# Expert layers: choosing beside weighing and collecting, norms turned over 128 columns with a power on GpSimd, weights in four tiles

## Chip, cores and metric

The kernel runs on one core of a Trainium2 chip. The time is device microseconds of one execution of the whole program; lower is better. A core has TensorE (PE; its weight loads are listed as PEld), VectorE (DVE), ScalarE (ACT), GpSimd (POOL) and SyncE (SP), whose queue issues the DMAs of this kernel.

## The reference, cut to what matters

Four layers work on x of shape (4, 128, 64, 64), that is 4 images of 128 channels and 4096 tokens. Layers 2 and 3 end in a layer of experts each. Only these two are touched by the change. Here `t` is x as tokens (4, 4096, 128):

```
t = t + attention(_ln_t(t));  t = t + _ffn_ref(_ln_t(t))        # layers 2 and 3

def _ln_t(v, eps=1e-5): return (v - mean(v)) / sqrt(var(v) + eps)   # over 128 channels

def _ffn_ref(x, gate_w, gate_b, weight1, weight2):              # E=64 experts, H=512, K=8
    probs = softmax(x @ gate_w.T + gate_b, axis=1)              # over the 4096 tokens
    vals, idx = top_k(probs, 8)                                 # per image and expert
    pooled = sum_k x[idx_k] * vals_k
    h = gelu([pooled, 1] @ weight1[e]);  out = [h, 1] @ weight2[e]
    outputs[idx_k] += out * vals_k
```

Each expert picks its eight likeliest tokens of an image, sums them with their probabilities, runs a small network on the sum and adds the answer back to those tokens. The weights of a layer are 64 x (128 x 512 + 512 x 128) floats, 33.6 MB, each used once.

## The kernel before, in words

`expert_ffn` (L1703) is called twice, from the top function (L2057), once after layer 2's attention and once after layer 3's. The images stand in SBUF as four tiles of 128 channels by 4096 tokens. Two images make a pair `pr`; the 64 experts of one image and the 64 of the other fill the 128 partitions.

`weigh(pr)` (L1762) takes the tokens in 8 chunks of 512 columns, the two images of a pair in turn, so 16 steps `n`. `centred` multiplies by a centring matrix and squares on ScalarE. `deviation` multiplies the squares by a matrix of 1/128 (L91 is the line of every such matmul), so that every partition holds the variance; VectorE turns 64 partitions of 512 columns in blocks of 32 (L1782), ScalarE takes the square root of one column of each block (L1784), VectorE inverts (L1785) and turns a broadcast back (L1786) into `rs`, the inverse deviation of each token. `gates` multiplies the two images by the gates' weights and VectorE scales by `rs` (L1796) into `pick`.

`choose(pr)` (L1800) works on all 4096 columns of `pick` at once: add the bias (L1803), the eight largest (L1805), exponential with its sum on ScalarE (L1809), share of the sum (L1812), the eight largest again (L1814), replace these by zero in a copy (L1816), subtract, so that only the eight remain (L1817), and multiply them by `rs` into `pick_rs` (L1818).

`collect(pr)` (L1820) turns, chunk by chunk, `pick_rs` and both images so that tokens are on partitions (12 transposes, three copies to SBUF), and sums picked tokens by matmuls into `pool`; its tail puts the sums into `pooled`.

The calls are weigh(0); choose(0); weigh(1) interleaved with collect(0); choose(1); collect(1). `run` steps generators in turn and `in_turn` shifts the stages of a loop against each other by one step. That sets the order in which instructions are given; within `expert_ffn` a scheduler then sorts them on each engine by its own costs (only the attention of layer 2 has an order written out by hand).

Then come 16 groups of four experts: `hidden` (matmuls with `w1`, gelu), `turn_hidden`, `answer` (matmuls with `w2`), `place` (into `out_ps`). `expert_weights(g)` issues one DMA of 1 MB for `w1` and four of 256 KB for `w2`; each of the two has two buffers, groups 0 and 1 are loaded at the start and group g+2 once group g no longer needs its buffers. All DMAs stand in SP's queue in order, and an issue also waits for the DMA eight before it. At the end `out_s` is multiplied back onto the picked tokens and added to x (L1925).

`Common.layernorm_steps` (L99), used by the attention layers, has a turning over 128 columns already (L113 to L121): four variance matmuls of 32 rows, one turning of 128 columns, and four transposes on TensorE; its records serve as rows for such operations. GpSimd rows come from other layers too (L915, L1271, L1611).

Of the kernel before, what the change touches and what calls it, by code (L numbers as in the profile page):

```python
# [17 lines left out]
P = 128  # L18
# [3 lines left out]
CH = 512  # L22
# [8 lines left out]
class Common:  # L31
# [3 lines left out]
    def __init__(self, tc, pool):  # L35
# [6 lines left out]
        def const(name, shape, value):  # L42
            t = pool.tile(shape, F32, name=name)
            nc.vector.memset(t, value)
            return t
# [7 lines left out]
        nc.vector.tensor_tensor(self.center, self.ident, self.mean, ALU.subtract)  # L53
        self.eps5 = const("eps5", [P, 1], 1e-5)
        self.half_pi = const("half_pi", [P, 1], math.pi / 2)

# [33 lines left out]
    def mm(self, out, lhsT, rhs, start=True, stop=True):  # L90
        self.nc.tensor.matmul(out, lhsT, rhs, start=start, stop=stop)  # L91
# [7 lines left out]
    def layernorm_steps(self, out, terms, work, psum, affine=None, bufs=2):  # L99
# [22 lines left out]
        if affine is None:  # L122
            nc.vector.tensor_tensor(out, kept, vp, ALU.mult)
        else:
            nc.vector.scalar_tensor_tensor(kept, kept, g, vp, ALU.mult, ALU.mult)
            nc.gpsimd.tensor_scalar(out, kept, b, None, ALU.add)

    def later(self, f, *args, **kw):
# [971 lines left out]
def run(*parts):  # L1100
    for _ in in_turns(*parts):
        pass
# [600 lines left out]
def expert_ffn(K, xs, w, tag):  # L1703
# [10 lines left out]
    with ExitStack() as ctx:  # L1714
        pool = lambda name, bufs, **kw: ctx.enter_context(tc.tile_pool(reuse_waits="tile", name=f"{tag}_{name}", bufs=bufs, **kw))
        cst = pool("const", 1)
        wts = pool("wts", 2)
        tok = pool("tok", 1)
        work = pool("work", 2)
# [3 lines left out]
        def expert_weights(g):  # L1723
            es = slice(g * GE, (g + 1) * GE)
            w1 = wts.tile([P, GE, HID], F32, name="w1")
            nc.sync.dma_start(out=w1, in_=w["weight1"][es, 0:P, :].rearrange("e d h -> d e h"))
            w2 = wts.tile([P, GE, NHC, P], F32, name="w2")
            for e in range(GE):
                nc.sync.dma_start(
                    out=w2[:, e], in_=w["weight2"][g * GE + e, 0:HID, :].rearrange("(k p) o -> p k o", p=P)  # L1730
                )
            return w1, w2
# [8 lines left out]
        nc.sync.dma_start(out=b2, in_=w["weight2"][:, HID, :])  # L1741
        ahead = [expert_weights(g) for g in range(2)]
        gp = psum.tile([P, NE], F32, name="gate_ps", tag="mm")
# [15 lines left out]
        picks = [cst.tile([P, L], F32, name=f"pick{pr}") for pr in range(2)]  # L1759
        parts = {}  # L1760

        def weigh(pr):  # L1762

            pb = picks[pr]
            rs = parts[pr] = tok.tile([P, L], F32, name="rs")
            sqs = {}

            def src(n):
                return xs[2 * pr + n % 2][:, n // 2 * CH : n // 2 * CH + CH]

            def centred(n):
                xc = psum.tile([P, CH], F32, name="ln_xc", tag="mm")
                mm(xc, K.center, src(n))
                sqs[n] = work.tile([P, CH], F32, name="ln_sq")
                nc.scalar.activation(sqs[n], xc, AF.Square)

            def deviation(n):
                half, cols = slice(64 * (n % 2), 64 * (n % 2) + 64), slice(n // 2 * CH, n // 2 * CH + CH)
                vp = psum.tile([P, CH], F32, name="ln_var", tag="mm")
                mm(vp, K.mean, sqs[n])  # L1780
                vt = work.tile([P, CH // 32, 32], F32, name="ln_vt")
                nc.vector.transpose(vt[half].rearrange("p a b -> p (a b)"), vp[half])  # L1782
                sd = work.tile([P, CH // 32, 1], F32, name="ln_sd")
                nc.scalar.activation(sd[half], vt[half, :, 0:1], AF.Sqrt, bias=K.eps5[half])  # L1784
                nc.vector.reciprocal(sd[half], sd[half])  # L1785
                nc.vector.transpose(  # L1786
                    rs[half, cols].rearrange("p (a b) -> p a b", b=32), sd[half].to_broadcast([64, CH // 32, 32])
                )

            def gates(n):  # L1790
                if n % 2:
                    lp = psum.tile([P, CH], F32, name="logits", tag="mm")
                    for h in range(2):
                        mm(lp[64 * h : 64 * h + 64, :], gate, src(n - 1 + h))
                    cols = slice(n // 2 * CH, n // 2 * CH + CH)
                    nc.vector.tensor_tensor(pb[:, cols], lp, rs[:, cols], ALU.mult)  # L1796

            return in_turn(2 * NCH, centred, deviation, gates)

        def choose(pr):  # L1800

            pb, rs = picks[pr], parts[pr]
            nc.vector.tensor_scalar(pb, pb, gate_b, None, ALU.add)  # L1803
            top = work.tile([P, 8], F32, name="top")
            nc.vector.max(top, pb)  # L1805
            nmx = work.tile([P, 1], F32, name="nmx")
            nc.vector.tensor_scalar(nmx, top[:, 0:1], -1.0, None, ALU.mult)
            tot = work.tile([P, 1], F32, name="tot")
            nc.scalar.activation(pb, pb, AF.Exp, bias=nmx, accum_out=tot)  # L1809
            rt = work.tile([P, 1], F32, name="rt")  # L1810
            nc.vector.reciprocal(rt, tot)
            nc.vector.tensor_scalar(pb, pb, rt, None, ALU.mult)  # L1812
            top = work.tile([P, 8], F32, name="top")
            nc.vector.max(top, pb)  # L1814
            ws = parts[pr] = tok.tile([P, L], F32, name="pick_rs")
            nc.vector.match_replace(ws, top, pb, 0.0)  # L1816
            nc.vector.tensor_tensor(pb, pb, ws, ALU.subtract)  # L1817
            nc.vector.tensor_tensor(ws, pb, rs, ALU.mult)  # L1818

        def collect(pr):  # L1820
# [27 lines left out]
            ps = work.tile([P, P], F32, name="pool_s")  # L1848
            nc.vector.tensor_copy(ps, pl)
            tp = psum.tile([P, P], F32, name="pool_t", tag="mm")  # L1850
# [10 lines left out]
        run(weigh(0))  # L1861
        choose(0)
        run(weigh(1), collect(0))
        choose(1)
        run(collect(1))


# [5 lines left out]
        def hidden(g):  # L1873
            w1, _ = ahead[g]
            hp = psum.tile([P, HID], F32, name="hid_ps", tag="mm")
            for j in range(GE):
                mm(hp[group(j), :], pooled[:, NB * (g * GE + j) : NB * (g * GE + j) + 32], w1[:, j, :], start=True, stop=False)
            for j in range(GE):
                mm(hp[group(j), :], one(g * GE + j), b1, start=False, stop=True)
            hid = hids[g] = work.tile([P, HID], F32, name="hid", tag="tok0")  # L1880
            nc.scalar.activation(hid, hp, AF.Gelu)
# [8 lines left out]
        def answer(g):  # L1890
# [8 lines left out]
            nc.vector.tensor_copy(a, ap)  # L1899
            if g + 2 < NG:  # L1900
                ahead.append(expert_weights(g + 2))

# [12 lines left out]
        for pr in range(2):  # L1915
            os_ = work.tile([P, P], F32, name="out_s")
            nc.vector.tensor_copy(os_, ops[pr])
            for c in range(NCH):
# [215 lines left out]
```

## Time and profile before

| what | value |
|---|---|
| median of 3 runs | 9885.43 us (9885.13 to 9886.97) |
| profiled execution, its time | 9881.09 us |
| its span | 9879.3 us |
| mean granted clock of TensorE | 0.920 |
| busy share PE / DVE / ACT / POOL | 88% / 73% / 75% / 49% |
| first expert layer, from the gates' weights to the last x | 8786 to 9132 us |
| attention of layer 3 | 9132 to 9517 us |
| second expert layer | 9517 to 9868 us |

The profile is one execution. Its rows give, for a group of instructions, the line, the engine, the operation with output and inputs, the count, busy time and the mean of one, and then the idle time just before them and what ended it. The timeline gives start, duration and idle time of single instructions, the stretches give busy time of each engine between two moments, the granted clock of TensorE (1 is full) and what the DMA engines moved. The second expert layer, in the stretch view (us, PE, PEld, DVE, ACT and POOL busy, clock, DMA share, GB/s), by the same stages as those that the prediction shows of the first:

```profile
9517.30:9568.00 50.70, 42.98 (x99) 13.28 (x99) 32.54 (x59) 15.70 (x34) 0.25 (x2) 0.94 0.22 66
9568.00:9600.70 32.70, 0.00 (x0) 0.00 (x0) 27.19 (x10) 5.08 (x3) 0.00 (x0) 0.54 0.00 0
9600.70:9667.00 66.30, 59.59 (x321) 30.52 (x321) 38.08 (x67) 24.97 (x50) 0.00 (x0) 0.97 0.00 1
9667.00:9698.30 31.30, 0.00 (x0) 0.00 (x0) 27.17 (x10) 3.80 (x2) 0.00 (x0) 0.54 0.00 0
9698.30:9728.00 29.70, 27.79 (x231) 21.04 (x233) 6.12 (x10) 9.90 (x18) 0.00 (x0) 0.91 0.01 1
9728.00:9847.00 119.00, 96.61 (x1088) 42.05 (x1088) 16.01 (x34) 9.89 (x17) 0.00 (x0) 0.76 0.83 248
```

### The profile page before, as it was taken

To read this page: it belongs to the slowest core of one execution; us is meant where nothing else is said; L and a number is where in the kernel's file an instruction comes from. 1 tells how busy PE (TensorE), PEld (TensorE's weight loads), DVE (VectorE), ACT (ScalarE), POOL (GpSimd) and SP (SyncE) were. 2 spreads that over 40 slices of the span, in tenths; PEclk is the share of its full clock that TensorE was granted. 3 is DMA by queue.
4 is the path that set the end of the run, shared out by engine and by line. 5 is a ranking of instruction groups with operands and counts; after the bars stand their busy time and mean duration, and the time that the engine had idled before them with its cause. 6 is when DMAs were issued, how large, how long until landed. Compare 5 with 4: busy or idle time off the path is not lost.

```text
span 9879.3 us, 187787 instructions
## 1 busy us (share of the span) xinstructions
PE 8736.1 (88%) x74074; PEld 3348.6 (34%) x74074; DVE 7220.5 (73%) x7877; ACT 7410.6 (75%) x10669; POOL 4802.8 (49%) x3175
## 2 busy tenths in 40 slices
PE   5888888888869999989999989999989999967776
PEld 2222222244523333333333333333333333333433
DVE  2889897988658888758888758888758888743463
ACT  3766767654359999879999879999879999841531
POOL 1677676765435555455555455555455555420000
PEclk8887878889979999989999989999989999988997
DMA  4524435223121221231111131211131211124004
GB/s 116 124 69 118 97 83 125 67 76 88 46 70 40 40 40 41 48 94 39 40 39 41 46 97 39 40 40 39 44 101 39 39 40 39 40 93 121 1 18 154
DMA packets 575731, 635.31 MB, mean 64 GB/s; under 512 B 113080, under 2 KB 369152, under 8 KB 573824
## 3 DMA queue, kind: packets, MB, share of 16 engines
q1 hardware_dynamic: 574848, 623.30, 25.6%
q8 instruction: 584, 9.57, 0.4%
q14 instruction: 299, 2.45, 0.1%
HBM read 446.84 MB, written 109.07 MB: 56 GB/s over the span
## 4 chain that ended last, share of the span: by engine, by line
PE 69%; DVE 10%; POOL 6%; ACT 5%; DMA 4%; issue 3%; SPq 2%; DVEq 0%; POOLq 0%; ACTq 0%
PE ctx_ps L91 27%; PE acc_ps L91 13%; PE score L91 11%; PE conv L91 4%; DVE hs L912 3%; POOL hs L916 3%; PE ln_xc L91 2%; PE y_ps L91 2%; DVE hs L901 2%; PE xc_ps L91 1%; DMA w<-in_L_ffn_weight 1%; PE ln_var L91 1%; PE b_ps L91 1%; PE hid_ps L91 1%; PE kv L91 1%
## 5 line engine op out<-in xcount | busy, mean ns | idle before, releaser
L1535 ACT ACTIVATE ex<-score 128x1024 f32<-128x1024 f32 x5120 | 4925.4, 1036 | 218.5 <-PE score L91 125.7
L91 PE MATMUL ctx_ps<-ex,qt 128*32 128x512 f32 x20480 | 2733.9, 606 | 19.9 <-DVE ctx L1469 19.9
L1484 POOL TENSOR_TENSOR folded<-ex 128x1024 f32<-128x1024 f32 x512 | 1224.2, 2391 | 2101.5 <-ACT ex L1535 1836.6
L1541 DVE STREAM_TRANSPOSE turned<-ex 128x1024 f32<-128x1024 f32 x1536 | 1885.8, 1228 | 329.1 <-ACT ex L1535 328.7
L1517 DVE STREAM_TRANSPOSE turned<-ex 128x1024 f32<-128x1024 f32 x1532 | 1842.4, 1203 | 0.0
L91 PE MATMUL acc_ps<-turned,turned_v 128*32 128x256 f32 x24576 | 1769.5, 379 | 3.1 <-POOL qt L1229 2.3
L912 DVE TENSOR_TENSOR_SCAN hs<-decay,carry,hs 128x512 f32<-128x512 f32 x1024 | 1245.7, 1266 | 193.6 <-ACT decay L908 180.1
L91 PE MATMUL score<-queries,keys 32*128 32x512 f32 x10240 | 1335.3, 497 | 44.0 <-POOL queries L1219 37.9
L91 PEld LDWEIGHTS acc_ps<-turned,turned_v 128*32 128x32 f32 x24576 | 800.9, 110 | 1476.5 <-issue 1323.8
L916 POOL TENSOR_TENSOR hs<-hs,c_sb 128x1024 f32<-128x1024 f32 x512 | 1207.3, 2358 | 81.4 <-DMA c_sb<-c_d 40.3
L908 ACT ACTIVATE decay<-dt,a_neg 128x512 f32<-128x512 f32 x1024 | 693.0, 689 | 662.5 <-DVE hs L912 653.3
L91 PEld LDWEIGHTS score<-queries,keys 32*128 32x128 f32 x10240 | 512.6, 182 | 1139.2 <-ACT ex L1535 780.9
L1347 POOL TENSOR_TENSOR turned_v<-v,quarter 128x1024 f32<-128x1024 f32 x256 | 612.4, 2393 | 265.7 <-PE acc_ps L91 225.0
L91 PE MATMUL y_ps<-hs,pair 128*64 128x512 f32 x2048 | 661.5, 773 | 33.6 <-POOL hs L916 33.6
L1485 POOL TENSOR_TENSOR quarters<-folded 128x512 f32<-128x512 f32 x512 | 657.7, 1285 | 40.2
L91 PEld LDWEIGHTS ctx_ps<-ex,qt 128*32 128x32 f32 x20480 | 406.4, 108 | 654.7 <-issue 598.7
L901 DVE TENSOR_TENSOR hs<-dtx,b_ps 128x2048 f32<-128x2048 f32 x256 | 580.1, 2266 | 55.9 <-PE b_ps L91 31.6
L91 PE MATMUL b_ps<-dbc,state 32*64 32x512 f32 x1024 | 343.2, 752 | 233.4 <-DVE hs L901 233.2
L1535 ACT ACTIVATION_READ_ACCUMULATOR ex<-score 128x1 f32 x2048 | 435.9, 213 | 0.0
L915 POOL COPY carry<-hs 128x2 f32<-128x2 f32 x512 | 98.1, 192 | 673.4 <-DVE hs L912 652.0
L1469 DVE COPY ctx<-ctx_ps 128x512 f32<-128x512 f32 x256 | 176.9, 691 | 329.3 <-PE ctx_ps L91 327.0
L1526 DVE TENSOR_REDUCE dacc<-quarters 128x2 f32<-128x512 f32 x508 | 327.1, 644 | 0.0
(371 smaller groups left out, 9016.1 us busy)
## 6 DMA issues: line engine op xcount, KB each, us to landing
c_sb<-c_d SPq DMA_DIRECT2D x512, 128.0 KB
queries<-head_d SPq DMA_DIRECT2D x1024, 64.0 KB
keys<-head_d SPq DMA_DIRECT2D x1024, 64.0 KB
under<-image_d SPq DMA_DIRECT2D x192, 264.0 KB
dt<-dt SPq DMA_DIRECT2D x128, 256.0 KB
dtx<-dtx SPq DMA_DIRECT2D x128, 256.0 KB
v<-value_d SPq DMA_DIRECT2D x1024, 32.0 KB
w<-in_L_ffn_weight SPq DMA_DIRECT2D x32, 1024.0 KB
```

The costliest lines, as they stand in the source:

```text
L91: self.nc.tensor.matmul(out, lhsT, rhs, start=start, stop=stop)
L901: nc.vector.tensor_tensor(hs, dtx2, bb.unsqueeze(1).to_broadcast([P, NQ, CH]), ALU.mult)
L908: nc.scalar.activation(ex, dt2[:, q, :], AF.Exp, scale=a_neg[:, q, g : g + 1])
L912: nc.vector.tensor_tensor_scan(hs[:, q, :], decays[q - 2 * i], hs[:, q, :], carry[:, g, q : q + 1], ALU.mult, ALU.add)
L916: nc.gpsimd.tensor_tensor(hs[:, two, :], hs[:, two, :], cs.unsqueeze(1).to_broadcast([P, 2, CH]), ALU.mult)
L1347: nc.gpsimd.tensor_tensor(t, v.unsqueeze(2).to_broadcast([P, 4 * BT, 4, HD]), quarter.unsqueeze(1).to_broadcast([P, 4 * BT, 4, HD]), ALU.mult,
L1484: nc.gpsimd.tensor_tensor(hs, exs[:, :, 0], exs[:, :, 1], ALU.add)
L1485: nc.gpsimd.tensor_tensor(qs, hs[:, :, 0 : CH // 2], hs[:, :, CH // 2 :], ALU.add)
L1517: nc.vector.transpose(*upright)
L1526: nc.vector.tensor_reduce(at, qs, AX.X, ALU.add)
L1535: nc.scalar.activation(ex, sps[p], AF.Exp, scale=scale, accum_out=sums[:, t : t + 1] if summed else None)
L1541: nc.vector.transpose(*upright)
```

## The change

Four things change, all in `expert_ffn`. Norms: `deviation` works on a chunk of both images; eight variance matmuls of 32 rows put the variances of 2 x 512 tokens on 128 partitions by 256 columns, one turning on VectorE, an add of the epsilon, a power of -1/2 on GpSimd and a broadcast copy there; a new stage `spreaded` transposes on TensorE and copies to `rs` on ScalarE. Choices: the bias goes into the exponential, the share into the copies `pool_s` and `out_s`, the second maximum is an exponential of the first; subtraction and product go chunk by chunk, the last two chunks on GpSimd; the function yields between its steps and runs beside weigh(1) and collect(0). Weights: one tile for both weights of a group, four such tiles, which also serve `rs` and `ws`; groups 1, 2 and 3 are loaded around collect(1), then g+4 after group g. A constant `minus_half` is added, and a helper `inverse_root`, which nothing calls.

```diff
         def weigh(pr):
-            rs = parts[pr] = tok.tile([P, L], F32, name="rs")
+            rs = parts[pr] = store.tile([P, L], F32, name="rs", tag="rs", bufs=2)
...
+            def deviation(c):
+                vp = psum.tile([P, 2, P], F32, name="ln_var", tag="mm")
+                for h, sq in enumerate(sqs.pop(c)):
+                    for k in range(4):
+                        mm(vp[32 * k : 32 * k + 32, h, :], K.mean[:, 0:32], sq[:, P * k : P * k + P])
+                vt = work.tile([P, 8, 32], F32, name="ln_vt")
+                nc.vector.transpose(vt.rearrange("p a b -> p (a b)"), vp.rearrange("p h s -> p (h s)"))
+                sd = work.tile([P, 4, 2], F32, name="ln_sd")
+                nc.vector.tensor_scalar(
+                    sd.rearrange("p k h -> p h k"), vt.rearrange("p (h k) i -> p h k i", h=2)[:, :, :, 0], 1e-5, None, ALU.add
                 )
+                flat = sd.rearrange("p k h -> p (k h)")
+                nc.gpsimd.tensor_tensor(flat, flat, K.minus_half[:, 0:8], ALU.pow)
+                wide = sds[c] = work.tile([P, 4, 2, 64], F32, name="ln_wide")
+                nc.gpsimd.tensor_copy(wide, sd.unsqueeze(3).to_broadcast([P, 4, 2, 64]))
+
+            def spreaded(c):
+                wide = sds.pop(c)
+                rp = psum.tile([P, CH], F32, name="ln_rs", tag="mm")
+                by_block = rp.rearrange("p (g b i) -> p b g i", b=4, i=32)
+                for k in range(4):
+                    nc.tensor.transpose(by_block[:, k], wide[:, k].rearrange("p h e -> p (h e)"), K.ident)
+                nc.scalar.copy(rs[:, c * CH : (c + 1) * CH], rp)
...
+            return in_turn(NCH, centred, deviation, spreaded, gates)
         def choose(pr):
             pb, rs = picks[pr], parts[pr]
-            nc.vector.tensor_scalar(pb, pb, gate_b, None, ALU.add)
             top = work.tile([P, 8], F32, name="top")
             nc.vector.max(top, pb)
...
+            yield
+            peak = work.tile([P, 1], F32, name="peak")
+            nc.vector.tensor_scalar(peak, top[:, 0:1], gate_b, None, ALU.add)
+            nc.vector.tensor_tensor(peak, gate_b, peak, ALU.subtract)
             tot = work.tile([P, 1], F32, name="tot")
...
+            nc.scalar.activation(top, top, AF.Exp, bias=peak)
+            nc.scalar.activation(pb, pb, AF.Exp, bias=peak, accum_out=tot)
+            nc.vector.reciprocal(shares[pr], tot)
+            yield
+            ws = store.tile([P, L], F32, name="ws", tag="b")
             nc.vector.match_replace(ws, top, pb, 0.0)
...
+            yield
+            for c in range(NCH):
+                cols = slice(c * CH, c * CH + CH)
+                engine = nc.vector if c < 6 else nc.gpsimd
+                engine.tensor_tensor(pb[:, cols], pb[:, cols], ws[:, cols], ALU.subtract)
+                engine.tensor_tensor(rs[:, cols], pb[:, cols], rs[:, cols], ALU.mult)
+                if c % 2:
+                    yield
...
         run(weigh(0))
-        choose(0)
-        run(weigh(1), collect(0))
-        choose(1)
+        run(weigh(1), choose(0))
+        run(choose(1), collect(0))
+        ahead[1] = expert_weights(1)
+        ahead[2] = expert_weights(2)
         run(collect(1))
+        ahead[3] = expert_weights(3)
...
         def expert_weights(g):
             es = slice(g * GE, (g + 1) * GE)
-            w1 = wts.tile([P, GE, HID], F32, name="w1")
+            t = store.tile([P, L], F32, name="w", tag=("a", "b", "rs", "rs")[g % 4], bufs=1 + g % 4 // 2)
+            w1 = t[:, 0 : GE * HID].rearrange("p (e h) -> p e h", e=GE)
...
-            if g + 2 < NG:
-                ahead.append(expert_weights(g + 2))
+            if g + 4 < NG:
+                ahead[g + 4] = expert_weights(g + 4)
```

## The prediction

> **What bounds the kernel now.** I read the page first: the span is 9879.3 us in a profiled execution of 9881.09 us (1.8 us lie around the span), and the shown runs have a median of 9885.43 us, 4.3 us above it. The program's instruction order on every engine is the same in both kernels up to the first expert layer, and again in the attention between the two expert layers, except for one small constant. So only two stretches count: 8762 to 9132 us and 9517 to 9868 us. I cut the first with the busy-time-by-stretch view (us, then PE, PEld, DVE, ACT, POOL busy, clock, DMA share, GB/s):
>
> ```profile
> 8786.50:8837.40 50.90, 43.19 (x100) 13.35 (x99) 32.44 (x58) 14.42 (x33) 0.00 (x0) 0.94 0.27 78
> 8837.40:8869.90 32.50, 0.00 (x0) 0.00 (x0) 27.05 (x10) 5.08 (x3) 0.00 (x0) 0.54 0.00 0
> 8869.90:8936.70 66.80, 59.66 (x321) 30.53 (x321) 38.14 (x68) 23.69 (x49) 0.00 (x0) 0.97 0.00 1
> 8936.70:8969.30 32.60, 0.00 (x0) 0.00 (x0) 27.16 (x10) 5.08 (x3) 0.00 (x0) 0.54 0.00 0
> 8969.30:8998.30 29.00, 27.06 (x227) 20.37 (x227) 6.14 (x11) 9.84 (x18) 0.00 (x0) 0.93 0.00 1
> 8998.30:9113.50 115.20, 95.23 (x1088) 41.94 (x1088) 15.74 (x33) 9.95 (x17) 0.00 (x0) 0.76 0.86 259
> ```
>
> The rows are weigh(0), choose(0), weigh(1) with collect(0), choose(1), collect(1), and the 16 groups of experts. In both choices TensorE does nothing for 32.5 us: VectorE alone carries the stage. Where weighing runs, TensorE is the limit (43 of 51, 60 of 67 us). The second expert layer repeats it: 50.7, 32.7, 66.3, 31.3, 29.7 and 119.0 us. The waits of these stretches, then four-microsecond stretches and the timeline inside the groups:
>
> ```profile
> PE tok_t L1830 <- DVE pick_rs L1818: 68.4, 2, 34.7
> ```
> ```profile
> PE hid_ps L91 <- DMA w<-in_L_ffn_weight: 18.6, 6, 4.1
> ```
> ```profile
> 9016.00:9020.00 4.00, 0.58 (x4) 0.23 (x8) 0.00 (x0) 0.00 (x0) 0.00 (x0) 0.72 1.14 334
> ...
> 9024.00:9028.00 4.00, 4.00 (x47) 2.43 (x40) 0.98 (x2) 0.00 (x0) 0.00 (x0) 0.50 0.43 129
> ```
> ```profile
> 9048.57 0.66 PE L91 MATMUL out_ps<-ans,spread 128*64 128x128 f32 x8
> ...
> 9051.26 1.35 PE L91 MATMUL hid_ps<-w,pooled 128*32 128x512 f32 x8 [2.03 <-DMA w<-in_L_ffn_weight]
> ...
> 9052.55 1.93 PE L91 MATMUL hid_ps<-b,ident 64*32 64x512 f32 x8
> ...
> 9057.90 1.04 PE L91 MATMUL out_ps<-ans,spread 128*64 128x128 f32 x8
> ...
> 9058.87 1.06 PE L91 MATMUL hid_ps<-w,pooled 128*32 128x512 f32 x8
> ```
>
> TensorE waits for weights every second group, and then works at half clock (1.93 us for what takes 1.06): the waits show 18.6 us, the half clock costs more. While TensorE works at half clock the loads stop (129 GB/s), since only two groups have a place. With loads queued they run at 330 GB/s (334, 326, 334, 336 in such stretches): 2.097 MB of a group take 6.35 us. At full clock a group costs TensorE 4.53 us (9005.61 to 10.14), at half clock 8.27 us (9019.42 to 27.69).
>
> **weigh(0).** A round of the loop is a chunk of 512 columns for two images. Before, on TensorE: 2 centrings of 1.02, 2 variances of 1.12, gates 1.08 = 5.36 us, measured 5.68. Now: centrings 2.04, eight variance matmuls of 32 rows by 128 columns 0.84 (four take 0.42 at L113), four transposes 0.65 (L121), gates 1.08 = 4.61 us. VectorE falls from about 4.0 us a round to 1.3 (one transpose of 128x256, between 0.31 for 128x128 and 0.71 for 64x512: 0.44; an add 0.15; the gates' multiply 0.69); ScalarE has two squares and a copy, 1.8 us. All that lies beside TensorE.
> The new wait is on the transposes of a round: they stand in TensorE's queue ahead of the next variances, centrings and gates, and need VectorE's transpose and add, then GpSimd's power and broadcast. Between a variance and that place lie centrings and gates, 3.12 us. The chain: 0.44 + 0.15 + power + 0.61 (a broadcast copy of that size, row below) + some 0.3 of handovers = 1.5 us + power. No row shows a power. Lower end 0.19 us (a GpSimd copy of 128x2, L915); upper end 3 us, an estimate from the GpSimd rows of 2.3 ns an element: a hundred such steps on 8 elements are 1.9 us, and I add half. It is nearest to the small two-input row:
>
> ```profile
> L1271 POOL TENSOR_TENSOR q<-q,cs 128x64 f32<-128x64 f32 x160 | 63.4, 396 | 12.1
> ...
> L1611 POOL COPY rc<-rd 128x512 f32<-128x512 f32 x32 | 19.5, 610 | 81.5 <-DVE rd L1609 81.5
> ```
>
> I take 0.4 us, so the cover holds by 1.2 us; at 3 us each round loses 1.4. The stage: the first transposes come about 8.9 us after the first centring (half clock until then, as before), six rounds of 4.61, the last two without centrings, 42.5 us in all. Saved: 8.
>
> **Choices beside weighing and collecting.** A choice sheds two passes of 2.35 us (bias, share) and one maximum of 4.43, the share going into two 128x128 copies that cost 0.29 either way. VectorE keeps maximum 4.43, match 4.5, and 12 of 16 chunk subtractions and products; four go to GpSimd (1.27 us each, 5.1, beside). ScalarE keeps its exponential of 3.9 and loses the square root and its table loads (1.28 each).
> A rule speaks against that split: the Trainium skill, GPSIMD Engine Reference, Engine selection and Specifications, leaves two-input elementwise work to VectorE and says that GpSimd contends with VectorE instructions that have two SBUF inputs. The trace shows such contention (minimum, median, maximum in ns; the minimum ran with GpSimd still, at 215.31):
>
> ```profile
> L130 DVE TENSOR_TENSOR dt<-sp_u,dt x32: 1192/1674/2036, 215.3 to 2520.0; 128x1024 f32<-128x1024 f32 x32
> ```
>
> By the row alone, 12 chunks of 0.61 are 7.3 us, slowed up to 1.7 times for 5 us: up to 9.8. All 16 on VectorE, as the rule wants, are 9.8 too. I take 9.8.
> VectorE's built order decides the overlap. choose(0) stands right behind weigh(0): maximum, first transpose of weigh(1), peak, second transpose, reciprocal (which waits for ScalarE's exponential), match, one gates' multiply, all 12 chunk operations, and only then the third transpose. From the end of weigh(0): maximum to 4.4, peak 5.4, exponential with table load to 10.2, match to 15, multiply 15.7, chunk operations to 25.5, transpose, add, power, broadcast to 28. TensorE has by then two rounds and most of a third, is out of work at about 16, and stands 12 us behind VectorE at its transposes. Left then: six transposes, five variances, four pairs of centrings, six gates = 22.7 us, 3 for a cold clock, 2 for the last chain: 56 us. choose(1) with collect(0): the eight copies of 0.69, maximum, match, 9.8 and small ones are 26 us of VectorE, with a short wait for the exponential; collecting alone takes 29.0 less its tail. Both give about 29. So 131.9 us (32.5 + 66.8 + 32.6) become 85 in the first layer, 130.3 in the second: 47 and 45 saved.
> collect(1) is as before, 29 us: nothing added; its VectorE has 6 of 29 us.
>
> **Weights in four tiles.** A tile now holds both weights of a group; three of the four are first used for rs and ws. Group 0 is loaded at the start, where x ends the wait as before (gates' weights at 8786): nothing. On SP's queue only weights stand behind the new waits: group 2 waits for the last rs transposes of collect(0), group 1 behind it, group 3 for those of collect(1). Groups 2 and 1, 12.7 us, hide under collect(1)'s 29; uncovered they would cost that. Group 3 starts where those transposes end, 5.9 us before the loop (8992.4 against 8998.3). From there the loads need never stop: when TensorE waits for group g, g-2 has been answered, so g to g+2 are queued. 13 groups x 6.35 = 82.6 us; 82.6 - 5.9 + 1.5 latency + 3.3 for the last answer = 81.5, and 1.5 for a cold clock: 83.
> On that clock: the Trainium skill, TensorE: Matmul & The Clock Gate, Part 1: The HAM clock gate, halves the clock after an idle window of about 3.4 us. The coming gaps, 6.35 - 4.53 = 1.8 us, would leave it full, and the loop 81.5. But the rows above halve it after 2.03 us; then a group costs 8.27 us now and then, the two groups of slack take that up, and the tail is 3 us longer, 84.5. I take the middle. Saved: 32 and 36.
> The constant's memset (0.1 us) lies under the start of the program; the unused helper costs nothing.
>
> **Sum.** First layer 8 + 47 + 32 = 87, second 8 + 45 + 36 = 89: 176 us. 9881.1 - 176 = 9705 for a profiled execution, and 4.3 more for the median: 9709.
>
> **Rivals.**
> - Power dearer than its cover (0.10): at 3 us, 1.4 us in each of the 8 rounds of weigh(0) and 6 later ones of weigh(1), two layers: 39, so 9748. For: no row prices it. Against: it works on 8 elements a partition.
> - Weights keep the old mean (0.09): at 259 GB/s a group takes 8.1 us, 13 take 105; the loop ends at 104 and saves 26 of the 68: 9751. For: that mean is all that the loop ever showed. Against: the stops coincide with half clock.
> - Better overlap (0.06): TensorE sets weigh(1) (40) and collect(0) (26): 19 less a layer, 9671. Against: twelve chunk operations in one block on VectorE.
> - Slower (0.03): the same place, power and broadcast on GpSimd become the pace of both weighings. 176 us are lost when each of some 15 rounds in two layers loses 5.9 us: power from about 7.5 us. At 10 us: 30 x 8.4 = 252, so 9709 + 252 = 9961.
> - The choices stay serial (0.02): 9709 + 92 less the shed passes (4 x 9.1) = 9765. Against: the built order interleaves them.
> - The likeliest (0.70): 9709, by itself 9680 to 9735.
>
> The range is 9675 to 9770: it takes in the two rivals above, and nearly all of the one below. Faster by over 0.2% (20 us, about what can be told from no change) 0.96, within it 0.01, slower 0.03.
>
> **What would show it.** weigh(0) in 43 us with the transposes waiting little for GpSimd; power near 0.4 us; in weigh(1) a TensorE wait of about 12 us at the third transposes with VectorE busy; in the groups a DMA share near 1, 330 GB/s, and a loop of about 83 us. Wrong: power over 1.6 us, loads under 300 GB/s, or subtractions far above 0.8 us beside GpSimd.

## The result, and the profile after

The changed kernel takes 9736.65 us in the median of 4 runs (9732.69 to 9744.07); the kernel before, run beside it, 9885.28 us. The ratio is 0.9848 with an interval of 0.9834 to 0.9863: 148.6 us less, where 176 were forecast. The profiled execution is the longest of the four, 9744.07 us with a span of 9742.2 us.

The first expert layer in the stretch view (us, PE, PEld, DVE, ACT and POOL busy, clock, DMA share, GB/s), cut at weigh(0); weigh(1) with choose(0); choose(1) with collect(0); collect(1); the groups:

```profile
8796.40:8841.10 44.70, 38.73 (x227) 14.83 (x227) 10.70 (x25) 14.23 (x24) 18.00 (x16) 0.89 0.17 46
8841.10:8897.50 56.40, 38.20 (x224) 14.64 (x222) 29.57 (x42) 19.40 (x28) 24.25 (x20) 0.83 0.00 1
8897.50:8929.60 32.10, 22.16 (x226) 19.50 (x224) 26.03 (x27) 12.52 (x19) 6.31 (x4) 0.83 0.35 109
8929.60:8958.30 28.70, 25.92 (x230) 19.38 (x230) 6.82 (x12) 9.97 (x19) 0.00 (x0) 1.00 0.28 78
8958.30:9047.80 89.50, 79.22 (x1088) 36.35 (x1088) 15.72 (x32) 9.99 (x17) 0.00 (x0) 0.92 0.98 293
```

The stages add up to 251.4 us where the six of before had 327.0. Against the forecast:

| stage | forecast | first layer | second layer |
|---|---|---|---|
| weigh(0) | 42.5 | 44.7 | 42.9 |
| weigh(1) with choose(0) | 56 | 56.4 | 56.9 |
| choose(1) with collect(0) | 29 | 32.1 | 31.5 |
| collect(1) | 29 | 28.7 | 28.3 |
| 16 groups | 83 | 89.5 | 92.5 |

The second layer fell from 329.7 to 252.1 us, so both together save 153 us by the profiles. The difference to the medians' 148.6 lies in layers whose instructions are those of before, and they scatter: over the profiles of this study the first expert layer begins anywhere between 8786.8 and 8806.6 us. So a layer is best compared by itself.

The waits of the whole execution (us in total, times, longest):

```profile
PE ln_rs L1809 <- POOL ln_wide L1802: 49.1, 27, 11.6
...
PE hid_ps L92 <- DMA w<-in_L_ffn_weight: 21.8, 17, 1.8
...
PE pool L92 <- DVE tok L1859: 19.3, 2, 9.7
```

TensorE's wait for the choices (68.4 us before) is gone. In its place it waits for GpSimd's broadcast ahead of the transposes, 49.1 us, and in collect(0) for VectorE, 19.3 us. For weights it waits more often than before (17 times, not 6), but never over 1.8 us. The timeline of TensorE in weigh(0), and then in weigh(1):

```profile
8814.94 0.66 PE L1809 MATMUL ln_rs<-ident,ln_wide 128*128 128x128 f32 x4 [0.32 <-POOL ln_wide L1802]
8815.53 0.64 PE L92 MATMUL ln_var<-ln_sq,mean 128*32 128x128 f32 x16
8816.10 1.98 PE L92 MATMUL ln_xc<-x,center 128*128 128x512 f32 x4
8818.02 1.08 PE L92 MATMUL logits<-x,gate 128*64 128x512 f32 x4
8819.41 0.66 PE L1809 MATMUL ln_rs<-ident,ln_wide 128*128 128x128 f32 x4 [0.32 <-POOL ln_wide L1802]
...
8848.66 1.11 PE L1809 MATMUL ln_rs<-ident,ln_wide 128*128 128x128 f32 x4 [3.52 <-POOL ln_wide L1802]
...
8871.28 1.11 PE L1809 MATMUL ln_rs<-ident,ln_wide 128*128 128x128 f32 x4 [11.49 <-POOL ln_wide L1802]
```

A round of weigh(0) is 4.47 us (8814.94 to 8819.41), and from the third on each holds a wait of 0.32: from the end of the variances to the transposes it takes 3.24 us (8816.17 to 8819.41), and the centrings and gates fill 2.93 of them. In weigh(1) the third transposes wait 11.49 us, as forecast, and the clock is halved behind it (1.11 us for what takes 0.66). What GpSimd does ahead of them, duration as minimum, median, maximum in ns, from the view of one line:

```profile
L1800 POOL TENSOR_TENSOR ln_sd<-ln_sd,minus_half x32: 1635/1636/1670, 8802.4 to 9552.9; 128x8 f32<-128x8 f32 x32
```

The power on 8 elements a partition takes 1.64 us; 0.4 was taken. The chunk operations, timeline of VectorE and GpSimd:

```profile
8856.17 2.95 POOL L1841 TENSOR_TENSOR pick<-pick,ws 128x512 f32<-128x512 f32 x2 [2.21 <-DVE ws L1836]
...
8856.54 3.13 DVE L1841 TENSOR_TENSOR pick<-pick,ws 128x512 f32<-128x512 f32 x2
...
8859.08 3.38 POOL L1842 TENSOR_TENSOR rs<-pick,rs 128x512 f32<-128x512 f32 x2
8859.59 3.41 DVE L1842 TENSOR_TENSOR rs<-pick,rs 128x512 f32<-128x512 f32 x2
```

Beside GpSimd's four, VectorE's first four take 6.5 us together. The other eight run at 0.60 apiece; from the end of the match (8856.0) to the last product (8867.8) it is 11.8 us, of which 0.6 is a gates' multiply.

Loads, in the timeline of SP's queue and in four-microsecond stretches:

```profile
8952.51 0.37 SPq L1733 DMA_DIRECT2D w<-in_L_ffn_weight  x1
...
8964.84 0.37 SPq L1733 DMA_DIRECT2D w<-in_L_ffn_weight  x1
```
```profile
8962.00:8966.00 4.00, 4.00 (x64) 1.70 (x60) 1.05 (x3) 0.60 (x1) 0.00 (x0) 1.00 0.03 9
...
9012.00:9016.00 4.00, 3.47 (x64) 1.99 (x60) 0.98 (x2) 0.60 (x1) 0.00 (x0) 1.00 1.12 336
```

Group 3's load is issued at 8952.51, as forecast 5.8 us before the loop. But group 4's follows at 8964.84 only, 6.5 us into the loop: group 3 has landed by 8961, and from then to this issue the DMA engines stand still (9 GB/s). From there they run at about 330 GB/s to the end.

### The profile page after: what moved, and what is told of

Read it like the earlier page. It is cut to its first block, busy times and chain, and to the rows that moved or that the text cites. A ratio compares the mean times of both kernels' runs of the same rounds, so it can differ in the third digit from the quotient of the medians.

```text
span 9742.2 us, 188843 instructions
## 1 busy us (share of the span) xinstructions
PE 8688.3 (89%) x74586; PEld 3347.3 (34%) x74586; DVE 7104.0 (73%) x7782; ACT 7404.1 (76%) x10635; POOL 4901.3 (50%) x3255
## 4 chain that ended last, share of the span: by engine, by line
PE 68%; DVE 10%; POOL 7%; ACT 5%; DMA 5%; issue 4%; SPq 1%; DVEq 0%; POOLq 0%; ACTq 0%
PE ctx_ps L92 27%; PE acc_ps L92 14%; PE score L92 11%; DVE hs L919 4%; PE conv L92 4%; POOL hs L923 3%; DVE hs L908 2%; PE y_ps L92 2%; PE ln_xc L92 1%; PE xc_ps L92 1%; PE b_ps L92 1%; DMA w<-in_L_ffn_weight 1%; PE kv L92 1%; ACT decay L915 1%; ACT L915 1%
## 5 line engine op out<-in xcount | busy, mean ns | idle before, releaser
L92 PE MATMUL y_ps<-hs,pair 128*64 128x512 f32 x2048 | 655.7, 768 | 32.1 <-POOL hs L923 32.1
```

## The experiments

Each kernel ran beside the kernel before on the same chip, and the chips differ by a few us, so the ratio to before is compared (0.001 is 9.9 us; the changed kernel has 0.9848). The last column is taken from the timeline of each profile: from VectorE's copy of the gates' weights to its last addition to x (8786.8 to 9134.2 us in the first layer of before), first and second expert layer.

The interval of a ratio reaches some 14 us to either side, so a difference of two ratios below about 20 us is not clear by itself; there the two layers decide. They scatter as well: the same instructions took 347.4 and 349.8 us in the kernel before, 351.2 and 344.5 with the constant.

| kernel | median us | ratio, 95% interval | the two layers, us |
|---|---|---|---|
| before | 9885.28 | 1 | 347.4, 349.8 |
| changed | 9736.65 | 0.9848, 0.9834 to 0.9863 | 272.1, 272.9 |
| choices in series | 9752.61 | 0.9862, 0.9847 to 0.9877 | 281.0, 279.9 |
| two whole tiles | 9892.59 | 1.0006, 0.9998 to 1.0014 | 343.1, 347.4 |
| old norms | 9773.41 | 0.9886, 0.9872 to 0.9899 | 288.7, 285.4 |
| multiply for power | 9717.48 | 0.9826, 0.9813 to 0.9839 | 262.5, 261.1 |
| two places | 9796.88 | 0.9905, 0.9891 to 0.9918 | 296.8, 295.3 |
| early release | 9738.21 | 0.9846, 0.9833 to 0.9860 | 271.8, 271.0 |
| chunks spread | 9740.12 | 0.9848, 0.9835 to 0.9862 | 270.8, 271.0 |
| chunks on VectorE | 9739.79 | 0.9848, 0.9835 to 0.9861 | 267.3, 270.9 |
| a further round | 9716.68 | 0.9828, 0.9814 to 0.9841 | 260.6, 258.8 |
| all beside | 9678.67 | 0.9787, 0.9774 to 0.9801 | 240.1, 239.1 |
| constant only | 9896.04 | 1.0004, 0.9998 to 1.0011 | 351.2, 344.5 |
| fewer loads | 9709.80 | 0.9817, 0.9800 to 0.9833 | 255.0, 255.8 |

**Choices in series.**

```diff
-        run(weigh(1), choose(0))
-        run(choose(1), collect(0))
+        run(choose(0))
+        run(weigh(1), collect(0))
+        run(choose(1))
```

> The changed kernel with the choices alone put back in series: choose(0) between weigh(0) and weigh(1), choose(1) after collect(0); shed passes, norms and four tiles stay. Theory (overlap is what the choices gain): a choice by itself is 4.4 (maximum) + 0.4 + 5.0 (exponential with table load) + 4.4 (match) + 11.3 (chunk operations beside GpSimd) = 26 us with TensorE still; two of them and about 61 us of weigh(1) with collect(0) are 113 us where the changed kernel needs 88: 25 us a layer, 9785 to 9795 us. Rival (most of the saving was the shed passes, the overlap only swaps one wait for another, as the 11.5 us wait of TensorE in weigh(1) hints): under 10 us a layer, 9757 us or less.

Measured: 14 us by the ratios, 8 a layer. The theory fell and the rival held, with under 10 us a layer. The stretches choose(0), weigh(1) with collect(0), and the rest of collect(1):

```profile
8834.90:8860.00 25.10, 8.38 (x41) 5.01 (x39) 20.94 (x19) 8.83 (x10) 6.73 (x4) 0.66 0.00 0
8860.00:8912.90 52.90, 46.67 (x409) 27.81 (x409) 15.74 (x35) 19.34 (x35) 17.97 (x16) 1.00 0.14 41
...
8938.00:8959.70 21.70, 19.17 (x189) 14.55 (x189) 6.03 (x11) 7.58 (x14) 0.00 (x0) 1.00 0.55 168
```

A choice by itself takes 25.1 us where before it took 32.5: the shed passes, less what the split over two engines costs, are worth 7.4 us a choice, 30 us in all, with no overlap. Weighing with collecting takes 52.9 instead of 66.8 (61 had been put into the expectation): the new norms are worth 14 us there. Overlap then turns 25.1 + 52.9 + 25.1 = 103 into 88.5, and gives 7 us of it back: in series collect(1) takes 21.7 us instead of 28.7, since its transposes of images go ahead during the choice. That is the 8 us a layer.

**Two whole tiles.** `tag="ab"[g % 2]`, group 1 loaded after choose(1), g+2 after group g.

> The changed kernel with two weight tiles in turn instead of four (group 0 at the start, group 1 after choose(1), then g+2 after group g). Theory (more places keep the loads running, so the loop takes what the loads take): the group loop goes back from 90 us to 115 to 120 us in each layer, loads near 255 GB/s over the loop, granted clock there about 0.76: 9790 us. Rival (the loop gained because its loads were ahead when it began, not by running through): only the start is lost, two loads of 6.35 us a layer, 9762 us.

Measured: all of the gain is lost, more than either said: the loop takes 162.3 us at a clock of 0.63, so this isn't the undoing that it was meant to be. The loads in SP's queue show why, the first of group 2 and of group 4:

```profile
8973.18 0.37 SPq L1733 DMA_DIRECT2D w<-in_L_ffn_weight  x1
...
8994.38 0.37 SPq L1733 DMA_DIRECT2D w<-in_L_ffn_weight  x1
```

Two groups in 21.2 us, so one each 10.6: answer(g) stands behind hidden(g+1) on TensorE, so with two tiles that are released whole, the load of g+2 is issued only once that of g+1 has landed and been used, and no two overlap. Before, the two weights of a group had places of their own, and a first weight was free after hidden(g).

**Two places.** Two tiles taken once, and their halves released one by one, as before the change.

```diff
-            t = store.tile([P, L], F32, name="w", tag=("a", "b", "rs", "rs")[g % 4], bufs=1 + g % 4 // 2)
+            if g < 2:
+                places[g] = store.tile([P, L], F32, name="w", tag="ab"[g])
+            t = places[g % 2]
...
-            if g + 4 < NG:
-                ahead[g + 4] = expert_weights(g + 4)
+            if g + 2 < NG:
+                ahead[g + 2] = expert_weights(g + 2)
```

> The changed kernel with two places for weights as before the change: a group's two weights each in a half of a tile of its own, released one by one (the run with two whole tiles released both at once, so that no load overlapped another: a load every 10.8 us). Theory (four places keep the loads running): the loop goes back to 115 to 119 us, 26 to 28 us a layer, 9788 to 9793 us. Rival (the loop gained by being ahead at its start): two loads of 6.35 us a layer, 9762 us or less.

Measured: 56 us by the ratios, 24.7 and 22.4 us by the layers: a little under the theory, and nearly twice what the rival's two loads could take. The loop has the time, clock and rate of before:

```profile
8953.50:9068.70 115.20, 95.10 (x1088) 41.58 (x1088) 15.77 (x33) 9.92 (x17) 0.00 (x0) 0.76 0.83 259
```

**Old norms.** `weigh` of before in the changed kernel.

> The changed kernel with the norms of before in weigh (two turnings of 64 partitions by 512 columns on VectorE, root on ScalarE, reciprocal on VectorE); choices beside and four tiles stay. Theory (the new norms matter twice, since they also free VectorE beside the choice): weigh(0) 51 us instead of 45, and weigh(1) with choose(0) is bound by VectorE, 8 rounds of 4.0 us and 28 us of choice, 62 to 66 us instead of 56: 12 to 16 us a layer, 9761 to 9769 us. Rival (weigh(1) is held by the block of chunk operations in either form): only weigh(0) is longer, 6 us a layer, 9749 us.

Measured: 38 us by the ratios, 16.6 and 12.5 us, so 29, by the layers; the theory holds. weigh(0), and weigh(1) with choose(0), where VectorE has 51 of 61 us:

```profile
8799.40:8852.60 53.20, 45.66 (x99) 13.83 (x99) 32.49 (x58) 14.41 (x33) 0.00 (x0) 0.89 0.12 36
8852.60:8913.80 61.20, 45.34 (x110) 14.78 (x109) 51.42 (x75) 21.13 (x38) 6.71 (x4) 0.86 0.00 0
```

**Multiply for power.** `ALU.pow` becomes `ALU.mult` in `deviation`, so that the inverse root is left out.

> The changed kernel with a multiply on GpSimd in place of the power (same operands, so the inverse root is left out and the output is not the reference's). Theory (the power of 1.64 us is four times what was taken and has eaten its cover): the GpSimd step falls to 0.2 to 0.4 us; TensorE no longer waits 0.3 us a round in weigh(0), and the rounds whose cover is short (the last two of each weighing, the one behind the chunk operations) get 1.3 us shorter each: 6 to 9 us a layer, 9719 to 9725 us. Rival (TensorE and its clock set the rounds, the power lies beside them): at most 2 us a layer, 9733 us or more.

Measured: 22 us by the ratios, 9.6 and 11.8 us by the layers: the theory, a little more than it said. The group of GpSimd's step over one layer (busy us, mean ns), and weigh(0):

```profile
L1800 POOL TENSOR_TENSOR ln_sd<-ln_sd,minus_half 128x8 f32<-128x8 f32 x16 | 3.2, 202 | 85.0 <-DVE ln_sd L1796 77.3 <-DVE peak L1829 7.7
```
```profile
8793.50:8831.00 37.50, 36.02 (x226) 14.15 (x226) 10.74 (x25) 14.23 (x24) 6.49 (x16) 0.94 0.16 47
```

0.20 us instead of 1.64, and a round of weigh(0) is 4.08 us with no wait: that is TensorE's own pace, where the prediction had 4.61. weigh(1) with choose(0) is 51.1 us, though TensorE's wait behind the block is 13.46 us there: TensorE only gets to it sooner.

**Early release.** The tile of groups 0, 4, 8 and 12 becomes two of half the size, one for each weight.

> The changed kernel with the tile of groups 0, 4, 8, 12 cut in two tiles of half the size, so that the first weight of group 4 can be loaded once hidden(0) is done, not after answer(0) as its whole tile. Theory (the loop is 6 us longer than forecast because the loads stand still between the landing of group 3 and the issue of group 4): the load of group 4 starts 4 to 5 us earlier against the start of the loop, the loop takes 85 to 86 us, 4 us a layer less, 9727 to 9730 us. Rival (TensorE at half clock or the rate of the loads sets the loop's end): the hole closes, the loop keeps its 90 us, 9735 us or more.

Measured: no difference (0.9846), 0.3 and 1.9 us by the layers. The hole closes where it was: group 4's first weight is issued at 8962.97, 1.1 us into the loop, where it was 6.5 in the changed kernel. But it comes back behind it. The second weight still waits for answer(0), and group 5, whose tile is whole, for answer(1):

```profile
8962.97 0.37 SPq L1738 DMA_DIRECT2D wa<-in_L_ffn_weight  x1
8968.34 2.02 SPq L1741 DMA_DIRECT2D wa<-in_L_ffn_weight  x4
8972.86 0.37 SPq L1738 DMA_DIRECT2D w<-in_L_ffn_weight  x1
```

Group 5 is issued 11.0 us into the loop, as in the changed kernel (8969.36 there). The loop takes 90.7 and 90.5 us. Neither account as written was whole: the hole is real, but not one release makes it; all four places are full when the loop begins.

**Fewer loads.** From group 4 on, only the first weight is loaded; the matmuls stay and take the second weights of groups 0 to 3 again.

> The changed kernel with only the first weight loaded from group 4 on (half the bytes; their second weights are those of the groups 0 to 3 again, so the answers are left wrong), the matmuls as they are. Theory (loads that begin only at answer(0), 6.9 us into the loop, and then take 6.35 us a group set the loop's end): at 3.2 us a group they fall behind TensorE's 4.5, TensorE waits for none and keeps its full clock, and the loop takes 76 to 78 us instead of 90, 9709 to 9713 us. Rival (TensorE's waits of under 2 us and its half clock are not made by the loads alone, or the handovers between the stages of a group are what it runs at): the loop keeps 85 us or more, 9727 us or more.

Measured: 31 us by the ratios, 17.1 us a layer; the theory holds, and the loop is shorter still than it said:

```profile
8960.10:9034.00 73.90, 72.52 (x1088) 33.78 (x1088) 15.75 (x34) 10.02 (x17) 0.00 (x0) 1.00 0.55 184
```

TensorE is busy for 72.5 of 73.9 us at full clock. With all loads the loop is bound by them: 6.5 us to answer(0), then 12 groups of 6.35 us, are 82.7; latency, the last answer and some half clock make the 89.5.

**Chunks on VectorE.** `engine = nc.vector`.

> The changed kernel with all 16 chunk operations of a choice on VectorE, none on GpSimd. Theory (beside GpSimd's four the first four of VectorE take 6.6 us instead of 2.4, so the split of 12 takes 11.3 us where 16 alone take 9.8): 1.5 us a choice less and no power queued behind GpSimd's, 6 us in all, 9729 to 9732 us. Rival (the split relieves VectorE, and 16 in a row are slower than 0.61 us each): the block takes 12 us or more, 9740 us or more.

Measured: the time can't tell (0.9848). The stretches can: weigh(1) with choose(0) takes 55.0 us (56.4) and choose(1) with collect(0) 30.5 (32.1), from match to the last product 10.3 us (11.8). That is the 1.5 us a choice of the theory; VectorE's 32 subtractions then all take the same (681 to 687 ns as listed, 0.60 us from one to the next).

**Chunks spread.** VectorE's order by hand; `paced` lets choose(0) go on by one step in every four stages of weigh(1).

```diff
-        run(weigh(1), choose(0))
+        with tc.manual_schedule(engines={mybir.EngineType.DVE}):
+            run(weigh(1), paced(choose(0), 4))
```

> The changed kernel with VectorE's order beside weigh(1) given by hand: one step of choose(0) to each round of weigh(1), so that the chunk operations come two chunks a round and not in one block (the reciprocal moves behind the exponential). Theory (TensorE loses 11.5 us at the third transposes, behind that block): the wait goes, weigh(1) with choose(0) takes 43 to 46 us instead of 56, 9711 to 9717 us. Rival (maximum and match of 4.4 us each and GpSimd's chunk operations then stand in front of a turning or a power in several rounds, and each takes back 2 to 4 us): under 5 us a layer, 9727 us or more.

Measured: no difference (0.9848), 1.3 and 1.9 us by the layers: the rival held. weigh(1) with choose(0), then TensorE's waits in it, and two of the rows behind them:

```profile
8829.30:8884.90 55.60, 39.72 (x224) 15.26 (x223) 28.51 (x42) 19.08 (x28) 25.68 (x20) 0.83 0.00 0
```
```profile
8836.78 1.12 PE L1809 MATMUL ln_rs<-ident,ln_wide 128*128 128x128 f32 x4 [3.60 <-POOL ln_wide L1802]
...
8847.72 0.42 PE L92 MATMUL ln_var<-ln_sq,mean 128*32 128x128 f32 x8 [0.39 <-ACT ln_sq L1785]
8851.39 0.66 PE L1809 MATMUL ln_rs<-ident,ln_wide 128*128 128x128 f32 x4 [3.25 <-POOL ln_wide L1802]
8858.18 2.08 POOL L1800 TENSOR_TENSOR ln_sd<-ln_sd,minus_half 128x8 f32<-128x8 f32 x1
8862.10 1.12 PE L1809 MATMUL ln_rs<-ident,ln_wide 128*128 128x128 f32 x4 [4.91 <-POOL ln_wide L1802]
```

The 11.5 us are gone. Of the three waits, the first, behind the maximum, was there before (3.52 us in the changed kernel); the other two, 8 us, are new. The second follows variances whose squares ScalarE's exponential of 3.7 us held back; in TensorE's order they stand right ahead of the transposes, so nothing covers the chain. The third is behind GpSimd's chunk operations, which hold back a power, to 8858.18, and then its broadcast. With a cover of 3 us, long steps on VectorE, ScalarE and GpSimd all reached TensorE, in one block or in pieces.

**A further round.** An empty stage between `deviation` and `spreaded`.

> The changed kernel with one empty stage between deviation and spreaded in weigh (and a third ln_wide), so that a round's transposes stand behind a whole further round of TensorE's work. Theory (power, turning and choice reach TensorE through one cover of 3.1 us, which the power of 1.64 us has used up; a round of 4.1 us more covers it): TensorE no longer waits for GpSimd in weigh(0), the wait behind the block of chunk operations in weigh(1) falls from 11.5 to about 7 us, a layer from the gates' weights to its last x takes about 262 us instead of 272, 9712 to 9718 us. Rival (the further stage only lengthens start and end of each weighing by a round): a layer keeps 270 us or more, 9733 us or more.

Measured: 20 us by the ratios, 11.5 and 14.1 us by the layers. The time is the theory's, and the waits for GpSimd in weigh(0) are gone: 36.9 us. One part of it fell: in weigh(1) the wait behind the block is not shorter.

```profile
8851.81 0.44 DVE L1794 STREAM_TRANSPOSE ln_vt<-ln_var 128x256 f32<-128x256 f32 x1
...
8863.60 0.16 DVE L1796 TENSOR_SCALAR ln_sd<-ln_vt 128x8 f32<-128x8 f32 x1
...
8866.20 1.11 PE L1809 MATMUL ln_rs<-ident,ln_wide 128*128 128x128 f32 x4 [13.47 <-POOL ln_wide L1802]
```

VectorE's order tells why. It turns the third round's variances ahead of the block, but adds the epsilon only behind all 12 chunk operations, 11.8 us later, and power and transposes wait for this add. So the further round could not help there, and the theory's 7 us were not put to the test. The gain is that of the multiply, within what can be told: with this order the further round hides the power, and nothing of the choice.

**All beside.** That round, all chunk operations on VectorE, the steps paced, and the chunk operations of choose(1) as a part of their own beside collect(1).

```diff
         run(choose(1), collect(0))
+        ahead[2] = expert_weights(2)
+        run(subtract(1), collect(1))
         ahead[1] = expert_weights(1)
-        ahead[2] = expert_weights(2)
-        run(collect(1))
```

> The changed kernel with the further round of the run before, all chunk operations on VectorE, one step of choose(0) to each round of weigh(1) by hand, and those of choose(1) beside collect(1) instead of collect(0). Theory (no single step of a choice is longer than the cover of 7 us, so weigh(1) runs at TensorE's pace, and collect(0) is free of 10 us of VectorE's work): weigh(1) 41 to 44 us instead of 56, collect(0) 24 to 27 instead of 32, a layer 246 to 252 us instead of 272, 9685 to 9697 us. Rival (as in the run with the chunks spread, each step moves to another wait): no more than the further round gives, 260 us a layer or more, 9712 us or more.

Measured: 60 us by the ratios, 32.0 and 33.8 us by the layers, 9678.67 us: faster than both kernels, and better than the theory's range. The first four of the five stretches shown of the changed kernel; the fifth, the loop, takes 89.9 us:

```profile
8799.20:8835.40 36.20, 35.56 (x227) 13.83 (x227) 10.82 (x25) 14.14 (x24) 18.04 (x16) 0.96 0.19 54
8835.40:8878.70 43.30, 35.66 (x225) 13.63 (x224) 30.18 (x46) 19.09 (x28) 18.00 (x16) 0.92 0.00 1
8878.70:8900.00 21.30, 20.52 (x224) 17.61 (x223) 17.86 (x21) 12.53 (x19) 0.00 (x0) 1.00 0.17 56
8900.00:8928.70 28.70, 25.93 (x234) 19.41 (x234) 13.37 (x23) 10.05 (x19) 0.00 (x0) 1.00 0.53 159
```

weigh(1) falls from 56.4 to 43.3 us and collect(0) from 32.1 to 21.3; collect(1) takes VectorE's work for nothing. Pacing without the round gave none of this, the round without pacing none in weigh(1) beyond the power. But three things differ in weigh(1) from the further round alone: the steps are spread, the order by hand keeps each add right behind its turning, and GpSimd has no chunk operations. Which of them it needs, and whether it needs the further round, no run here separates. TensorE's longest wait in it is 4.72 us, behind the match.

**Constant only.** The kernel before with `minus_half`.

> The kernel before with the constant minus_half alone (64 bytes a partition ahead of everything that follows in SBUF, used by nothing). Theory (layers 0 to 2, whose instructions are the same, ended 9.7 us later in the profile of the changed kernel by chance): the time is that of before, within 5 us of it. Rival (the moved addresses cost those 9.7 us in every execution): 0.1% slower, 9895 us.

Measured: 1.0004, 0.9998 to 1.0011. The theory, 3 to 4 us of no difference that can be told; the interval leaves up to 11 us open. In its profile the first expert layer begins at 8801.7 us, in that of before at 8786.8, in that of the kernel with the chunks spread at 8786.8 too, in that with two whole tiles at 8806.6, in all others between: single executions scatter by more than the 9.7 us asked about. Whether the moved addresses cost a few us stays open.

## Why the prediction was right, step by step

The direction held, and so did the order of sizes stage by stage, though not part by part, as the end of this section shows: 9736.65 us lies in the range, 28 us above the forecast and just above the likeliest case's own (9680 to 9735). 24 of these 28 are in the first three steps below.

- **"13 groups x 6.35 = 82.6 us; 82.6 - 5.9"** (16 us in two layers). The group time is right (the rate is 330 GB/s, and the loads bind, as fewer loads shows), and so is the start of group 3's load. What failed is "from there the loads need never stop". It argued from the state in which TensorE waits for a group; at the loop's start it waits for none. Groups 0 to 3 fill the four places, and the next is free at answer(0), 6.5 us into the loop. The stream that sets the end is 12 groups from there (82.7 us), not 13 from 5.9 us ahead of it (76.7): 6 us a loop, and half clock in the tail makes the rest. Early release shows that freeing one place earlier doesn't bring it back.
- **"I take 0.4 us, so the cover holds by 1.2 us"** (3 us by the stage, 22 by the runs). The power takes 1.64 us, within the bounds of 0.19 and 3, and the row of a small two-input step was the wrong neighbour: with a multiply, that row's kind, it takes 0.20. With 1.64 the sum's chain is 3.1 us, just its cover of 3.12; measured, the chain is 3.24 and the cover 2.93, since the listed durations overlap, so each round waits 0.32. The forecast of weigh(0) is only 2 us off because a second term was wrong the other way: a round of TensorE was put at 4.61 us and takes 4.08 (variances 0.64, not 0.84, and the listed durations overlap by some 0.3 us). With a power of 0.2 weigh(0) takes 37.5 us and weigh(1) with choose(0) 51.1. So that 42.5 and 56 us came out so near is luck, two errors of opposite sign in each, and the power costs 22 us of the whole time against a multiply, which the sum doesn't show.
- **"choose(1) with collect(0) ... both give about 29"** (6 us). VectorE's block is 11.8 us, not 9.8 (of which 0.6 is a multiply). GpSimd's four slow VectorE's first four to about 1.6 us each, 2.7 times their pace alone, not 1.7. The rule weighed against the split, of the Trainium skill, GPSIMD Engine Reference, Engine selection and Specifications, was right: all 16 on VectorE take 1.5 us a choice less. It mattered only in the stretches. The row of contention was misread in one point, without effect on the ratio of 1.7: with GpSimd still, at 215.31, the operation took 1224 ns, and the minimum of 1192 was another, partly beside GpSimd.
- **choose(0) beside weigh(1)**: 56 us and a wait of 12 us at the third transposes were forecast, 56.4 and 11.49 measured. Two readings of it failed. That the block made the loss: spread out, it is lost in other places. And the 47 us a layer were put down to the choices alone, 18 of them to shed passes (in the rival of serial choices) and so 28 to overlap. By the series, of 43 measured 15 are shed passes, 14 the norms in weigh(1), and overlap gives 15 and takes 7 back in collect(1). That rival put serial choices at 9765 us; in series they take 9752.61.
- **collect(1)** unchanged: right. **The granted clock** of the loop rose from 0.76 to 0.92. That the clock would halve now and then after gaps near 2 us, against the rule (the Trainium skill, TensorE: Matmul & The Clock Gate, Part 1: The HAM clock gate) of an idle window of 3.4 us, held. In TensorE's timeline of the loop, at the second of two waits 6.2 us apart, of 1.76 and 1.63 us, and the stretch with the granted clock:

```profile
9002.61 1.06 PE L92 MATMUL hid_ps<-w,pooled 128*32 128x512 f32 x8 [1.63 <-DMA w<-in_L_ffn_weight]
...
9004.86 1.93 PE L92 MATMUL ans_ps<-w,hid_u 128*32 128x128 f32 x32
```
```profile
9004.00:9008.00 4.00, 4.00 (x51) 2.27 (x44) 0.29 (x1) 0.60 (x1) 0.00 (x0) 0.53 1.08 353
```

The same 32 matmuls take 1.08 us in the group before. But not every such wait does it: of the 11 waits of 1.4 to 1.8 us in the two loops, 4 were followed by half clock. These four halvings begin at 9004.27, 9028.17, 9663.05 and 9700.59, on a grid of 3.41 us (7, 186 and 11 steps from one to the next). In the step of this grid ahead of each, TensorE was busy for 1.68 to 1.78 us; of the 40 steps after which the clock stayed full, one had 1.65 and all others 1.88 or more. So what goes with a halving here is a step of which TensorE works about half, and not the length of one wait. With fewer loads and no gaps the clock stays at 1.00.

By undoing one part at a time, the weights are worth 56 us by the ratios and 47 by the layers (68 forecast), the norms 38 and 29 (16 forecast, since their share of weigh(1) was booked under the choices), the overlap 14 and 16 (some 56 forecast), and the shed passes, by 4 x 7.4, about 30; no run undid these alone. Each part was taken away with the others in place, so they need not add up to the 149. The rivals named did not decide: the power was dearer, though by half of what that rival took, and weights did not keep the old mean.

What stays open: the few us in the layers before, and which of the changes of the last faster kernel, all beside, make weigh(1) short.

## What to carry to other kernels

A wait that follows a choice of order, like the 11.5 us here, is not yet its cause: work out how much independent work lies between an operation and its consumer, and compare that with the longest single step on any engine of the chain. If a step is longer, look at each engine's order too: here neither spreading nor a deeper pipeline helped alone, since GpSimd's operations or an add left behind the block kept TensorE waiting, and together, with these two out of the way, they did. When places for loads are counted, count them at the start of the loop, where all of them are full, and not only in its steady state. And a sum that comes out right is not yet a right sum: weigh(0) and weigh(1) each hid two errors of opposite sign.

## What was not expected of the hardware

- GpSimd's power costs 1.64 us for 128 x 8 elements, eight times a multiply of the same tile (0.20 us), and beside VectorE's two-input operations up to 2.08 us (in the kernel with the chunks spread).
- Two-input operations of 512 columns on VectorE take 0.60 us by themselves and about 1.6 us while GpSimd does the same; GpSimd's go from 1.27 to 1.7. Together the two engines did 4 + 4 such operations in 6.8 us; VectorE alone does 8 in 4.8.
- The clock can halve though TensorE never waits longer than 1.8 us and works three quarters of the time: it did behind 4 of 11 such waits, those that left TensorE some 1.7 us of work in a step of 3.41; one further step with as little work was not followed by it.
